# The code search reads x as loaded: the norm's scale goes into the codes of each sample, its shift into the row of code norms

## The chip, the cores and the metric

The kernel runs on one core of a Trainium2 chip. The metric is the device time of one execution in microseconds (us). An execution is timed as a whole; a profiled execution also shows every instruction of the five engines: TensorE (PE, with its weight loads shown apart as PEld), VectorE (DVE), ScalarE (ACT), GpSimd (POOL) and SyncE (SP), which here only issues DMAs.

## What is computed

The input x has 16 samples of 64 x 64 tokens with 256 channels, in f32. Four layers follow each other, each on the group norm of what the layer before left. The change touches the first one: each normed token is replaced by the nearest of 1024 code vectors, and that code is added to x.

```python
def _gn(v, G=32, eps=1e-5):
    g = v.reshape(B_, H_, W_, G, C_ // G)
    m = jnp.mean(g, axis=(1, 2, 4), keepdims=True)
    s = jnp.var(g, axis=(1, 2, 4), keepdims=True)
    return ((g - m) / jnp.sqrt(s + eps)).reshape(v.shape)
...
    dis = sum(xf * xf, axis=-1) + sum(embeddings * embeddings, axis=0) - 2.0 * matmul(xf, embeddings)
    indices = jnp.argmin(dis, axis=-1)
    quantized = jnp.take(embeddings.T, indices, axis=0)
...
    x = x + _L0_conv_ref(_gn(x), embeddings)
    x = x + _L1_conv_ref(_gn(x), ...)   # attention along rows, sigmoid
    x = x + _L2_conv_ref(_gn(x), ...)   # a gate by a softmax over 4096 x 4096 outer products
    x = x + _L3_conv_ref(_gn(x), ...)   # linear attention, then a layer norm
```

The norm is one scale s and one shift m for each sample and group of 8 channels, so a normed token is (x - m) s.

## The kernel before, in words

**Stages.** A sample passes through generators: `stats0` (loads the sample's x, channels on partitions, in 8 chunks of 512 tokens, and takes the norm's mean and variance), `stage1` (the search), `layer1`, `rows2`, `stage2` and `gate2` (the third layer), `stage3` (the fourth). A planner at the end of the file gives every generator a start time and a length in units of one sample and resumes, step by step, whichever is due first. In the middle of the run the search of one sample so lies beside the attention of the sample before, the exponentials of an earlier one, and so on. What the planner decides is the order in which the program names its instructions, which is their priority. A scheduler then gives each engine one fixed list; an engine takes its list strictly in order and waits where an operand is not there yet. Lines marked `tc.high_priority` are pulled ahead.

**The norm.** `gn_finish` ends every norm with a small chain: a weight on PE for the group means, the variance into `scale` on ACT (L276), minus the mean into `nmean` on ACT (L278), then on POOL the power -1/2 (L279) that makes `scale` the norm's s, and `nbias` = `nmean` x `scale` (L281). All three have one number for each channel.

**Constants.** The codes are loaded once into `e_raw` (256 x 1024 as two halves of 128 channels, 1 MB). ACT makes `e2`, twice the codes, which stays in SBUF for the whole run (L176); DVE and PE make `ne2`, minus the squared length of each code, repeated on all partitions.

**The search.** `stage1` goes through the 8 chunks. For a chunk, `load` fetches x (tile `xt`, three buffers); `norm` makes on ACT, for each half of the channels, the normed tile `xn` (L331) and its square `sq` (L334), then PE sums the squares of each token (L340), and after a copy on ACT (L345), a transpose (L347) and a copy on DVE (L352) minus the squared length of each token lies in `nx2`. For each of the 4 blocks of 128 tokens ACT writes `nn` = `ne2` + `nx2` (L381, 128 x 1024), PE multiplies `xn` with `e2` into the two-bank tile `pd` (L386, two halves of the codes times two halves of the channels), DVE adds the two and takes the maximum (L392), finds its place (L397), and POOL gathers that code from DRAM and adds it to the tokens (L398). `back` transposes the sum on PE (L361), ACT copies it over `xt` (L364), DVE takes the next norm's statistics, and the chunk is stored (L367). `norm` of a chunk is named after the third block of the chunk before, and `load` after its fourth block, two chunks ahead.

**Queues.** SP issues most loads and stores in one list, those of the search among them (L321, L325), and the loads of `stats0` (L302). Stores of `stage1` are issued by ACT.

Of the kernel before, what the change touches and what calls it, by code (L numbers as in the profile page):

```python
# [9 lines left out]
F32 = mybir.dt.float32  # L10
BF16 = mybir.dt.bfloat16
U32 = mybir.dt.uint32
AF = mybir.ActivationFunctionType
ALU = mybir.AluOpType
AX = mybir.AxisListType

P = 128
C = 256
NK = C // P
# [4 lines left out]
CW = CH * P  # L24
# [3 lines left out]
CODES = 1024  # L28
# [13 lines left out]
def kernel(  # L42
# [7 lines left out]
    nc = tc.nc  # L50
# [3 lines left out]
    const = ctx.enter_context(tc.tile_pool(name="const", bufs=1))  # L54
# [4 lines left out]
    s1p = ctx.enter_context(tc.tile_pool(name="s1p", bufs=2))  # L59
# [4 lines left out]
    dram = ctx.enter_context(tc.tile_pool(name="dram", bufs=2, space=bass.MemoryType.DRAM))  # L64
# [3 lines left out]
    def bank(name):  # L68
        return ps_m.tile([P, 512], F32, tag="pm", name=name)

    def wide(name):
        return ps_w.tile([P, 1024], F32, tag="pw", name=name)
# [99 lines left out]

    e_raw = s2p.tile([P, NK, CODES], F32, tag="x0b", name="e_raw", bufs=2)
    nc.sync.dma_start(out=e_raw, in_=emb.rearrange("(k p) n -> p k n", p=P))
    e2 = const.tile([P, NK, CODES], F32, name="e2")
    nc.scalar.mul(e2, e_raw, 2.0)  # L176
    e_sq = s2p.tile([P, NK, CODES], F32, tag="x2b", name="e_sq", bufs=2)
    nc.vector.tensor_tensor(e_sq, e_raw, e_raw, ALU.mult)
    ne2 = const.tile([P, CODES], F32, name="ne2")
    for hf in range(2):  # L180
        pe = bank(f"pe_{hf}")
        for k in range(NK):
            nc.tensor.matmul(
                pe, lhsT=neg_mat, rhs=e_sq[:, k, hf * 512 : (hf + 1) * 512],
                start=(k == 0), stop=(k == NK - 1),
            )
        nc.scalar.copy(ne2[:, hf * 512 : (hf + 1) * 512], pe)

    def load_wfg(t):
        nc.sync.dma_start(out=t[:, :, 0:CK], in_=wf.rearrange("(k p) n -> p k n", p=P))  # L190
        nc.sync.dma_start(out=t[:, :, CK : 2 * CK], in_=wg.rearrange("(k p) n -> p k n", p=P))
# [48 lines left out]
    for n in range(2):  # L240
        t = const.tile([P, CH, 2, ROW], F32, name=f"blk_{n}")
# [4 lines left out]
    for n in range(4):  # L246
        t = const.tile([P, 8], F32, name=f"m8_{n}")
# [4 lines left out]
    def stats_tile(kind, name):  # L252
        return small.tile([P, NK, NCHUNK, 6], F32, tag=f"gn_st{kind}", name=name, bufs=1)

    def chunk_stats(st, xt, ch):
        for k in range(NK):
            nc.vector.bn_stats(st[:, k, ch, :], xt[:, k, :])  # L257
# [33 lines left out]
                engine.tensor_scalar(v, v, scale[:, k : k + 1], None, ALU.mult)  # L291


    norm0 = {}

    def stats0(b):
        tag = f"s0_{b}"
        st = stats_tile(0, f"st_{tag}")
        src = xT[b].rearrange("(k p) n -> p k n", p=P)
        for ch in range(NCHUNK):  # L300
            xt = xb.tile([P, NK, CW], F32, tag="xb", name=f"xs_{tag}_{ch}")
            nc.sync.dma_start(out=xt, in_=src[:, :, ch * CW : (ch + 1) * CW])  # L302
            chunk_stats(st, xt, ch)
            yield 1.5
        with tc.high_priority(offset=URGENT):
            norm0[b] = gn_finish(st, "n0", b)
        yield 2


    x1_d, norm1 = {}, {}  # L310

    def stage1(b):
        tag = f"s1_{b}"
        scale, _, nbias = norm0.pop(b)
        src = xT[b].rearrange("(k p) n -> p k n", p=P)
        tok = x[b].rearrange("(t p) c -> p t c", p=P)
        xt, xc, xn, nx2, pxt = {}, {}, {}, {}, {}

        def load(ch):
            xt[ch] = xa.tile([P, NK, CW], F32, tag="xa", name=f"xt_{tag}_{ch}")  # L320
            nc.sync.dma_start(out=xt[ch], in_=src[:, :, ch * CW : (ch + 1) * CW])  # L321

        def tokens(ch):
            xc[ch] = s1p.tile([P, CH, C], F32, tag="xc", name=f"xc_{tag}_{ch}")
            nc.sync.dma_start(out=xc[ch], in_=tok[:, ch * CH : (ch + 1) * CH, :])  # L325

        def norm(ch):
            xn[ch] = s1p.tile([P, NK, CW], F32, tag="xn", name=f"xn_{tag}_{ch}")
            sq = s1p.tile([P, NK, CW], F32, tag="t4", name=f"sq_{tag}_{ch}", bufs=3)
            for k in range(NK):  # L330
                nc.scalar.activation(  # L331
                    xn[ch][:, k, :], xt[ch][:, k, :], AF.Identity, bias=nbias[:, k : k + 1], scale=scale[:, k : k + 1]
                )
                nc.scalar.activation(  # L334
                    sq[:, k, :], xt[ch][:, k, :], AF.Square, bias=nbias[:, k : k + 1], scale=scale[:, k : k + 1]
                )
            px = bank(f"px_{tag}_{ch}")
            for t in range(CH):
                for k in range(NK):
                    nc.tensor.matmul(  # L340
                        px[32 * t : 32 * t + 32, :P], lhsT=neg32, rhs=sq[:, k, t * P : (t + 1) * P],
                        start=(k == 0), stop=(k == NK - 1),
                    )
            xrow = small.tile([P, P], F32, tag="xrow", name=f"xrow_{tag}_{ch}", bufs=1)
            nc.scalar.copy(xrow, px[:, :P])  # L345
            pxt[ch] = bank(f"pxt_{tag}_{ch}")
            nc.tensor.transpose(pxt[ch][:, :P], xrow, ident)  # L347

        def norm_rows(ch):
            px = pxt.pop(ch)  # L350
            nx2[ch] = small.tile([P, CH], F32, tag="x2", name=f"nx2_{tag}_{ch}")
            nc.vector.tensor_copy(nx2[ch], px[:, :P].rearrange("p (t n) -> p t n", n=32)[:, :, 0])  # L352

        st1 = stats_tile(1, f"st1_{tag}")
        x1_d[b] = []

        def back(ch):
            for k in range(NK):
                pt = bank(f"pt_{tag}_{ch}_{k}")
                for t in range(CH):  # L360
                    nc.tensor.transpose(  # L361
                        pt[:, t * P : (t + 1) * P], xc[ch][:, t, k * P : (k + 1) * P], ident
                    )
                nc.scalar.copy(xt[ch][:, k, :], pt)  # L364
            chunk_stats(st1, xt[ch], ch)
            d = dram.tile([P, NK, CW], F32, tag=f"x1_{ch}", name=f"x1_{tag}_{ch}")
            nc.scalar.dma_start(out=d, in_=xt.pop(ch))  # L367
            x1_d[b].append(d)

        load(0)  # L370
        load(1)
        norm(0)
        norm_rows(0)
        tokens(0)
        yield 4
        for ch in range(NCHUNK):
            for t in range(CH):
                T = ch * CH + t

                nn = s1p.tile([P, CODES], F32, tag="t4", name=f"nn_{tag}_{T}", bufs=3)  # L380
                nc.scalar.activation(nn, ne2, AF.Identity, bias=nx2[ch][:, t : t + 1])  # L381
                pd = wide(f"pd_{tag}_{T}")
                for hf in range(2):
                    cols = slice(hf * 512, (hf + 1) * 512)
                    for k in range(NK):
                        nc.tensor.matmul(  # L386
                            pd[:, cols], lhsT=xn[ch][:, k, t * P : (t + 1) * P], rhs=e2[:, k, cols],
                            start=(k == 0), stop=(k == NK - 1),
                        )

                m8 = m8s[T % 4]
                nc.vector.tensor_tensor_reduce(  # L392
                    out=nn, in0=pd, in1=nn, scale=1.0, scalar=-3.0e38, op0=ALU.add, op1=ALU.max,
                    accum_out=m8[:, 0:1],
                )
                i8 = small.tile([P, 8], U32, tag="i8", name=f"i8_{tag}_{T}", bufs=4)
                nc.vector.max_index(i8, m8, nn)  # L397
                nc.gpsimd.indirect_dma_start(  # L398
                    out=xc[ch][:, t, :], out_offset=None,
                    in_=emb_rows, in_offset=bass.IndirectOffsetOnAxis(ap=i8[:, 0:1], axis=0),  # L400
                    compute_op=ALU.add,
                )
                yield 4
                if t == 1 and ch > 0:
                    back(ch - 1)
                    yield 2
                if t == 2 and ch + 1 < NCHUNK:
                    norm(ch + 1)
                    yield 2
                if t == 3:  # L410
                    if ch + 1 < NCHUNK:
                        norm_rows(ch + 1)
                        tokens(ch + 1)
                    if ch + 2 < NCHUNK:
                        load(ch + 2)
        back(NCHUNK - 1)
        with tc.high_priority(offset=URGENT):
            norm1[b] = gn_finish(st1, "n1", b)
        yield 3
# [492 lines left out]
    for _ in stats0(0):  # L912
        pass
    queue = [(start, n) for n, (start, _, _, _) in enumerate(tasks)]
    heapq.heapify(queue)
    while queue:
        now, n = heapq.heappop(queue)
        _, length, gen, total = tasks[n]
# [40 lines left out]
```

## Time and profile before

| | before |
|---|---|
| median of 3 executions | 5701.88 us (5696.69 to 5706.75) |
| the profiled execution | 5709.26 us |
| its span, first to last instruction | 5707.6 us |
| mean TensorE clock granted | 0.941 of full speed |
| moved by DMA | 991.87 MB, 174 GB/s on the mean |

How to read it: busy time is what the engine spent in instructions, without waiting; the mean of a group is the duration of one instruction, and since an instruction starts while the one ahead is still draining, the busy time of a group can be less than count times mean. "Idle before" is what the engine waited just ahead of a group, and behind the arrow stands who ended the wait. The chain of waits is followed back from the last instruction; in this profile its pieces reach back to about 1229 us from the start.

An f32 matmul of the source stands in the profile as two instructions: L386 is called 16 x 32 x 4 = 2048 times and has 4096 rows.

### The profile page before, as it was taken

What the parts mean: (1) busy time and instruction counts of PE and PEld (TensorE: products, weight loads), DVE (VectorE), ACT (ScalarE), POOL (GpSimd) and SP (SyncE); (2) the same over time, 40 slices, a digit from 0 to 9 for tenths busy, and PEclk for the clock granted to TensorE, in tenths of its full rate; (3) what the DMA queues carried; (4) which work ended last, traced back from release to release, by engine and by line L of the source; (5) the groups of instructions that cost most, each with busy time, mean ns of one, the idle gap of its engine ahead of it and who ended that gap; (6) DMA issues with size and microseconds to landing.
All of it is one profiled execution on the core that took longest, in us unless ns stands there. A gap on an engine that the chain in (4) does not pass through costs nothing.

```text
span 5707.6 us, 71918 instructions
## 1 busy us (share of the span) xinstructions
PE 5070.7 (89%) x24911; PEld 2999.1 (53%) x24911; DVE 5046.3 (88%) x7186; ACT 4578.7 (80%) x6578; POOL 1929.1 (34%) x1203
## 2 busy tenths in 40 slices
PE   8978899889999999999989999899999999997777
PEld 3534455445555565554645555564555545564444
DVE  6489798999999999998999999999898998988982
ACT  4478587978889798887978888798887878888873
POOL 3123233323333334334333333333333333321332
PEclk9988999989999999999999999999999999997888
DMA  6453835655666757566575756757475674745544
GB/s 187 141 158 93 265 112 188 176 161 177 191 188 176 212 160 198 175 190 186 170 205 163 187 188 177 203 161 218 143 193 172 184 207 142 203 153 160 158 137 92
DMA packets 453763, 991.87 MB, mean 174 GB/s; under 512 B 50456, under 2 KB 198808, under 8 KB 445208
## 3 DMA queue, kind: packets, MB, share of 16 engines
q1 hardware_dynamic: 320272, 750.88, 39.7%
q0 software_dynamic: 92160, 134.26, 15.5%
q10 hardware_dynamic: 40968, 102.13, 4.6%
q8 instruction: 198, 3.24, 0.2%
q14 instruction: 165, 1.35, 0.1%
HBM read 684.07 MB, written 303.04 MB: 173 GB/s over the span
## 4 chain that ended last, share of the span: by engine, by line
PE 34%; DVE 19%; ACT 13%; issue 6%; POOL 3%; DMA 3%; ACTq 0%; SPq 0%; POOLq 0%; DVEq 0%
PE pd_s L386 11%; DVE ex_s L631 7%; ACT ex_s L628 6%; PE ph_l L476 3%; DVE i_s L397 3%; PE pqv_s L762 2%; PE pxo_s L874 2%; PE pk_s L745 2%; ACT nn_s L381 2%; DVE nn_s L392 2%; POOL qv_s L780 1%; PE po_l L516 1%; PE pz_s L835 1%; DVE st_s L257 1%; DVE xg_g L686 1%
## 5 line engine op out<-in xcount | busy, mean ns | idle before, releaser
L631 DVE CUSTOM_DVE_ANT_0 ex_s<-ex_s,x2b 128x2048 f32<-128x2048 f32 x1024 | 2364.2, 2315 | 77.0 <-ACT ex_s L628 75.1
L628 ACT ACTIVATE ex_s<-x0b,nmax_s,x_r 128x2048 f32<-128x2048 f32 x1024 | 2137.9, 2088 | 80.8 <-DVE num_s L631 77.8
L386 PE MATMUL pd_s<-e,xn_s 128*128 128x512 f32 x4096 | 2008.5, 625 | 71.6 <-DVE m L392 61.5
L398 POOL DMA_INDIRECT xc_s<-in_emb_rows,i_s x512 | 1160.6, 2267 | 1794.2 <-DVE i_s L397 1255.3
L386 PEld LDWEIGHTS pd_s<-e,xn_s 128*128 128x128 f32 x4096 | 763.4, 198 | 855.4 <-issue 705.3
L392 DVE CUSTOM_DVE_ANT_0 nn_s<-pd_s,nn_s 128x1024 f32<-128x1024 f32 x512 | 619.7, 1213 | 137.4 <-PE pd_s L386 100.5
L381 ACT ACTIVATE nn_s<-ne,nx_s 128x1024 f32<-128x1024 f32 x512 | 580.4, 1143 | 55.9 <-DVE nx_s L352 27.5
L397 DVE FIND_INDEX8 i_s<-m,nn_s 128x8 uint32<-128x1024 f32 x512 | 623.5, 1219 | 0.0
L476 PE MATMUL ph_l<-wh_l,xt_l 128*128 128x256 f32 x2048 | 536.1, 399 | 68.0 <-DVE xt_l L521 42.6
L762 PE MATMUL pqv_s<-wqv_s,xk_s 128*128 128x256 f32 x2048 | 488.7, 380 | 0.0
L476 PEld LDWEIGHTS ph_l<-wh_l,xt_l 128*128 128x128 f32 x2048 | 386.6, 196 | 193.1 <-issue 65.9
L762 PEld LDWEIGHTS pqv_s<-wqv_s,xk_s 128*128 128x128 f32 x2048 | 388.7, 191 | 120.2 <-issue 59.8
L780 POOL TENSOR_TENSOR qv_s<-qv_s,qm_s 128x512 f32<-128x512 f32 x128 | 216.1, 1688 | 640.0 <-DVE qm_s L779 329.3
L874 PE MATMUL pxo_s<-qo_s,wctx_s 128*128 128x512 f32 x512 | 279.5, 630 | 18.5 <-DVE qo_s L854 18.1
L736 POOL TENSOR_TENSOR qv_s<-qv_s,qd_s 128x512 f32<-128x512 f32 x128 | 186.1, 1454 | 324.7 <-DVE qd_s L735 189.8
L516 PE MATMUL po_l<-blk,h_l 128*128 128x128 f32 x2048 | 286.1, 291 | 3.6 <-DVE m L392 2.9
L516 PEld LDWEIGHTS po_l<-blk,h_l 128*128 128x128 f32 x2048 | 263.1, 202 | 42.2 <-issue 22.8
L884 POOL DMA_DIRECT2D out<-y_s x128 | 118.9, 929 | 479.3 <-ACT lrs_s L845 235.2
L745 PE MATMUL pk_s<-xk_s,wk_s 128*128 128x512 f32 x512 | 259.0, 626 | 0.0
L846 POOL TENSOR_TENSOR lrs_s<-lrs_s,mhalf 128x4 f32<-128x4 f32 x128 | 199.0, 1555 | 173.1 <-ACT lrs_s L845 164.2
L361 PE MATMUL pt_s<-ident,xc_s 128*128 128x128 f32 x1024 | 157.6, 289 | 103.6 <-DMA xc_s<-in_emb_rows,i_s 70.0
L875 ACT ACTIVATE y_s<-pxo_s,xm_g 128x512 f32<-128x512 f32 x256 | 174.6, 683 | 91.3 <-PE pxo_s L874 90.6
(191 smaller groups left out, 7012.6 us busy)
## 6 DMA issues: line engine op xcount, KB each, us to landing
xs_s<-in_xT SPq DMA_DIRECT2D x128, 512.0 KB
xt_s<-in_xT SPq DMA_DIRECT2D x128, 512.0 KB
xc_s<-in_x SPq DMA_DIRECT2D x128, 512.0 KB
x_s<-xt_s ACTq DMA_DIRECT2D x128, 512.0 KB
xt_l<-x_s SPq DMA_DIRECT2D x128, 512.0 KB
x_l<-xt_l SPq DMA_DIRECT2D x128, 512.0 KB
xr_r<-x_l SPq DMA_DIRECT2D x128, 512.0 KB
xg_g<-x_l SPq DMA_DIRECT2D x128, 512.0 KB
```

Source lines behind the costliest of these rows:

```text
L381: nc.scalar.activation(nn, ne2, AF.Identity, bias=nx2[ch][:, t : t + 1])
L386: nc.tensor.matmul(pd[:, cols], lhsT=xn[ch][:, k, t * P : (t + 1) * P], rhs=e2[:, k, cols], start=(k == 0), stop=(k == NK - 1),)
L392: nc.vector.tensor_tensor_reduce(out=nn, in0=pd, in1=nn, scale=1.0, scalar=-3.0e38, op0=ALU.add, op1=ALU.max, accum_out=m8[:, 0:1],)
L397: nc.vector.max_index(i8, m8, nn)
L398: nc.gpsimd.indirect_dma_start(out=xc[ch][:, t, :], out_offset=None, in_=emb_rows, in_offset=bass.IndirectOffsetOnAxis(ap=i8[:, 0:1], axis=0),
L476: nc.tensor.matmul(ph[:, t, :], lhsT=X[:, k, t * P : (t + 1) * P], rhs=wh_n[:, k, :], start=(t % 2 == 0 and k == 0), stop=False, skip_grou ...
L516: nc.tensor.matmul(po[:, m : m + P], lhsT=h[:, t, k * P : (k + 1) * P], rhs=at[:, t, :, :].rearrange("p r i -> p (r i)"), start=True, stop ...
L628: nc.scalar.activation(ex, x0b, AF.Exp, bias=nmax[:, T : T + 1], scale=x01[:, T, 1:2], accum_out=den[:, h, T : T + 1])
L631: nc.vector.tensor_tensor_reduce(out=ex, in0=ex, in1=x2b, scale=1.0, scalar=0.0, op0=ALU.mult, op1=ALU.add, accum_out=num[:, h, T : T + 1],)
L745: nc.tensor.matmul(pk, lhsT=wk_n[:, k, :], rhs=xt[:, k, :], start=(k == 0), stop=(k == NK - 1))
L762: nc.tensor.matmul(pqv[:, j, :], lhsT=xt[:, k, t * P : (t + 1) * P], rhs=wqv_n[:, k, :], start=(j == 0 and k == 0), stop=False, skip_group ...
L874: nc.tensor.matmul(px, lhsT=wctx[:, 1, pr * P : (pr + 1) * P], rhs=qT, start=True, stop=True)
```

## The change

The search takes `xt`, x as loaded, as its stationary operand. With `ec` = 2 s e for each sample, the product with the normed x is x `ec` + `nmean` `ec`; the second part is a number for each code and is added to `ne2`, which makes the row `cn`. The squared lengths of the tokens are made as before, from `sq`.

- `e2` leaves SBUF. `e_raw` is doubled in place and stored once to DRAM (`e2_d`, issued by ACT).
- `scale_codes`, called in the last steps of `stats0`, loads `e2_d` into `ec` (1 MB, issued by SP; two buffers) and scales both halves on ACT.
- `code_row`, at the head of `stage1`, multiplies `nmean`, broadcast to 128 columns, with `ec` on PE (4 matmuls of 128 x 512) into two PSUM banks of the shared pool, and DVE adds `ne2` into `cn` (one buffer).
- The ACT instructions of L331 and the tile `xn` (two buffers of 512 KB) are gone.

```diff
-    e2 = const.tile([P, NK, CODES], F32, name="e2")
-    nc.scalar.mul(e2, e_raw, 2.0)
...
+    nc.scalar.mul(e_raw, e_raw, 2.0)
+    e2_d = dram.tile([P, NK, CODES], F32, tag="e2", name="e2_d", bufs=1)
+    nc.scalar.dma_start(out=e2_d, in_=e_raw)
...
+    def scale_codes(b):
+        tag = f"ec_{b}"
+        scale, nmean, _ = norm0[b]
+        ec = s1p.tile([P, NK, CODES], F32, tag="ec", name=tag)
+        nc.sync.dma_start(out=ec, in_=e2_d)
+        for k in range(NK):
+            nc.scalar.activation(ec[:, k, :], ec[:, k, :], AF.Copy, scale=scale[:, k : k + 1])
+        codes[b] = ec
+
+    def code_row(b):
+        tag = f"cn_{b}"
+        nmean, ec = norm0[b][1], codes[b]
+        cn = s1p.tile([P, CODES], F32, tag="cn", name=tag, bufs=1)
+        for hf in range(2):
+            cols = slice(hf * 512, (hf + 1) * 512)
+            pc = bank(f"p{tag}_{hf}")
+            for k in range(NK):
+                nc.tensor.matmul(
+                    pc, lhsT=nmean[:, k : k + 1].to_broadcast([P, P]), rhs=ec[:, k, cols],
+                    start=(k == 0), stop=(k == NK - 1),
+                )
+            nc.vector.tensor_tensor(cn[:, cols], pc, ne2[:, cols], ALU.add)
+        return cn
...
             norm0[b] = gn_finish(st, "n0", b)
-        yield 2
+        yield 1
+        scale_codes(b)
+        yield 1
...
+        cn, ec = code_row(b), codes.pop(b)
...
             for k in range(NK):
-                nc.scalar.activation(
-                    xn[ch][:, k, :], xt[ch][:, k, :], AF.Identity, bias=nbias[:, k : k + 1], scale=scale[:, k : k + 1]
-                )
                 nc.scalar.activation(
                     sq[:, k, :], xt[ch][:, k, :], AF.Square, bias=nbias[:, k : k + 1], scale=scale[:, k : k + 1]
                 )
...
-                nc.scalar.activation(nn, ne2, AF.Identity, bias=nx2[ch][:, t : t + 1])
+                nc.scalar.activation(nn, cn, AF.Identity, bias=nx2[ch][:, t : t + 1])
...
-                            pd[:, cols], lhsT=xn[ch][:, k, t * P : (t + 1) * P], rhs=e2[:, k, cols],
+                            pd[:, cols], lhsT=xt[ch][:, k, t * P : (t + 1) * P], rhs=ec[:, k, cols],
```

More of the change, by code (lines that the diff above doesn't have):

```diff
@@ L291, in scaled @@
                 engine.tensor_scalar(v, v, scale[:, k : k + 1], None, ALU.mult)
-    norm0 = {}
+    norm0, codes = {}, {}
+    def scale_codes(b):
[20 more added lines that the diff above has]
+        return cn
     def stats0(b):
@@ L316, in stage1 @@
         tok = x[b].rearrange("(t p) c -> p t c", p=P)
-        xt, xc, xn, nx2, pxt = {}, {}, {}, {}, {}
+        xt, xc, nx2, pxt = {}, {}, {}, {}
         def load(ch):
@@ L327, in norm @@
         def norm(ch):
-            xn[ch] = s1p.tile([P, NK, CW], F32, tag="xn", name=f"xn_{tag}_{ch}")
             sq = s1p.tile([P, NK, CW], F32, tag="t4", name=f"sq_{tag}_{ch}", bufs=3)
             for k in range(NK):
-                nc.scalar.activation(
-                    xn[ch][:, k, :], xt[ch][:, k, :], AF.Identity, bias=nbias[:, k : k + 1], scale=scale[:, k : k + 1]
-                )
                 nc.scalar.activation(
```

## The prediction

> **What bounds the kernel now.** I read three things in order: the busy shares, one long stretch in the middle, and the chain of waits through that stretch. First the shares of the whole span:
>
> ```profile
> PE 5070.7 (89%) x24911; PEld 2999.1 (53%) x24911; DVE 5046.3 (88%) x7186; ACT 4578.7 (80%) x6578; POOL 1929.1 (34%) x1203
> ```
>
> Three engines are nearly full. Next the table of stretches, whose columns are the length, then the busy time of PE, PEld, DVE, ACT and POOL, the granted clock, and DMA:
>
> ```profile
> 1500.00:4880.00 3380.00, 3109.56 (x15606) 1857.03 (x15606) 3136.08 (x4456) 2858.71 (x4109) 1243.43 (x741) 0.96 0.64 183
> ```
>
> This is ten samples at 338 us each. PE is at 92%, DVE at 93%, ACT at 85%: DVE idles 24 us per sample, PE 27, ACT 52. No engine is so full that its work alone sets the time. So I go to the chain of waits and add up its pieces between 1500 and 4880: PE 1481 us, DVE 862, ACT 576, 269 without a releaser, the rest POOL and DMA. Divided by the busy times above, a microsecond of work lies on the chain with 0.48 on PE, 0.27 on DVE and 0.20 on ACT. These three weights price work spread over the stretch. Work removed cannot be worth more than its own pieces on the chain until the order of the lists changes; work added at one place may cost all or nothing. I keep both as bounds.
>
> **What goes.** The normed tile is 256 ACT instructions. The groups (shapes, count, busy us, mean ns, idle time before and who ended it):
>
> ```profile
> L331 ACT ACTIVATE xn_s<-xt_s,nb_n,s_n 128x512 f32<-128x512 f32 x256 | 201.5, 806 | 41.5 <-DMA xt_s<-in_xT 24.8 <-PE pd_s L386 14.1 <-POOL nb_n L281 1.1
> L340 PE MATMUL px_s<-sq_s,neg 128*32 128x128 f32 x2048 | 120.2, 292 | 46.8 <-ACT sq_s L334 46.8
> L386 PE MATMUL pd_s<-e,xn_s 128*128 128x512 f32 x4096 | 2008.5, 625 | 71.6 <-DVE m L392 61.5 <-ACT xn_s L331 6.1 <-ACT h_l L485 2.2
> ```
>
> ACT loses 201.5 us of work, 12.6 per sample. By ACT's weight that is worth 0.20 x 201.5 = 40 us. The pieces of L331 that stand on the chain add up to only 17.4 us: mostly something else was as late. One such place, from the chain (start, us, what):
>
> ```profile
> 2033.87 0.82 ACT xn_s L331
> 2034.73 1.13 PE pd_s L386 x2
> ```
>
> The 14.1 us in which ACT waited for PE before it overwrote `xn` go too, but an idle ACT costs little: by its weight 3. What is late next? The matmuls of the search waited for `xn` only 6.1 us; the DVE maximum that frees their PSUM tile ended ten times as much idle time (61.5) and stays. The squares start one or two instructions sooner, since L331 stood ahead of them, and the sums of squares (L340), behind which PE idled 46.8 us, can gain up to that; but the list of PE is made anew, and will again put them close behind the squares. Between 17 and 43 I take the middle, **-30**.
>
> **What comes on PE.** 16 x 4 matmuls of 128 x 512 in f32. The profile splits each in two (L386: 2048 calls, 4096 rows), so 128 instructions. Their price is that of the search's own, which the chain shows eight at a time without a gap:
>
> ```profile
> 1950.81 3.63 PE pd_s L386 x8
> 1954.88 3.43 PE pd_s L386 x8
> ```
>
> That is 0.43 us each; with the mean over the run, 2008.5 / 4096, it is 0.49. So 55 to 63 us, I take 59, or 3.7 per sample. The broadcast stationary operand is no extra: L853 loads one too, and takes 142 ns against 198 in L386, under cover of the matmul ahead. The matmuls stand at the head of a sample, ahead of its first sums of squares and search matmuls, which wait behind them; `ec` and `nmean` have been ready for long by then, except in the first sample. If the 27 us in which PE idles per sample hid them all, they would cost nothing; if PE is the bound, 59. By the weight, 0.48 x 59 = **+28**.
>
> **What comes on DVE.** 32 additions from PSUM, 128 x 512. Nearest row, the same shape with one operand in PSUM:
>
> ```profile
> L837 DVE TENSOR_TENSOR qz_s<-pz_s,qo_s 128x512 f32<-128x512 f32 x128 | 88.0, 688 | 70.9 <-PE pz_s L835 68.2 <-ACT y_s L875 2.7
> ```
>
> 32 x 0.69 = 22 us; by the weight 0.27, **+6**, bounds 0 and 22. `cn` has one buffer, so an addition also waits for the last `nn` of the sample before; that `nn` runs on ACT ahead of the last maximum on DVE, which stands in front of the addition in the same list, so this wait is covered.
>
> **What comes on ACT and on the queues.** 32 scalings of 128 x 1024, priced by the writing of `nn`, which has the same size and also one operand per partition:
>
> ```profile
> L381 ACT ACTIVATE nn_s<-ne,nx_s 128x1024 f32<-128x1024 f32 x512 | 580.4, 1143 | 55.9 <-DVE nx_s L352 27.5 <-DVE i_s L397 26.6
> L557 ACT ACTIVATE wrow_n<-wrow_raw,s_n 128x12 f32<-128x12 f32 x32 | 8.0, 296 | 11.6 <-POOL s_n L279 11.4
> ```
>
> 32 x 1.13 = 36 us, by 0.20 **+7**. They add a wait: the scheduler puts them right behind the ACT instruction that feeds POOL's power (L276), so ACT stands until POOL answers, with the exponentials (L628) queued behind, and DVE waits for those. L557 waits in the same way for another norm, 11.4 us in 16 samples. I take that, 11 us, and by a weight between ACT's and one **+5**; if ACT waited as long as the longest landing of a 1 MB load on the chain (9.3 us, `x0b`) in every sample, it would be 149, which I hold for excluded in the middle, since the 1 MB load of `ec` is issued most of a sample ahead. That load waits on SP for the last search matmul of the sample before, and the loads behind it in SP's list wait too; it stands behind a load that already waits for the store of chunk 6, which needs gathers, transposes, copies and a store after all but the last search matmuls, so I take 0. 17 MB more on 992 are 1.7%, with the DMA engines 64% busy: 0.
>
> **The start.** Here nothing covers. The table of instructions in order of time (start, us, what):
>
> ```profile
> 22.95 1.10 SPq L321 DMA_DIRECT2D xt_s<-in_xT  x2
> 29.84 0.81 ACT L331 ACTIVATE xn_s<-xt_s,nb_n,s_n 128x512 f32<-128x512 f32 x1 [1.12 <-POOL nb_n L281]
> 38.58 1.23 DVE L392 CUSTOM_DVE_ANT_0 nn_s<-pd_s,nn_s 128x1024 f32<-128x1024 f32 x1 [1.28 <-ACT nn_s L381]
> ```
>
> Now the codes go through DRAM first. ACT's store stands behind small loads that it issues until 16 us and behind the doubling (1.9 us), so about 20; then a store and a load of 1 MB, about 6.5 each beside the chunks of x (the `x0b` loads on the chain take 5.5 to 9.3): 33. Scaling 2.3, the code row on PE 3.4, then sums of squares, transpose, `nn` as before (about 5 us): the first maximum at 44 in place of 38.6. **+5**, bounds 0 and 15.
>
> **Sum.** -30 + 28 + 6 + 7 + 5 + 5 = +21 us on the profiled execution of 5709.26, so 5730. The median of the runs is 7 us lower, 5701.88; with the same +21 it becomes **5723**.
>
> **A rule that weighs otherwise.** The Trainium skill, "Perfetto Trace Analysis", "Identifying the Most-Contended Engine", says to work on the engine with the highest occupancy, and to judge TensorE by its weight loads, since matmul busy time misleads. By weight loads PE is at 53% here, DVE is the engine, the code row on PE is free and the sum is -7. But the search matmuls come 0.43 us apart without a gap, so PE is truly occupied in these pieces, and I keep its weight. By either reading the engine that is relieved, ACT, is only the third.
>
> **Rivals.** (a) *Faster: ACT's relief counts full.* ACT ends about half of PE's idle time. If the pieces behind L331 give back 43 us and half of the 46.8 behind the squares, and the code row hides in PE's idle 27 us per sample at half its weight, the sum is -43 - 23 + 14 + 6 + 7 + 5 + 5 = -29: 5673. For it speaks PE's wait for the squares; against it, that L331 has only 17.4 us on the chain. It decides once the wait behind the squares shrinks by more than half.
> (b) *Slower: PE pays in full.* The code row opens each sample in a lump that all of the search waits behind, so 59 and not 28, and the removed work returns its 17: -17 + 59 + 6 + 7 + 5 + 5 = +65: 5767. It decides if PE's idle time per sample stays at 27 us. For it speaks PE's chain weight, the largest; against it, that gaps of PE lie all through the sample.
> (c) *The lists change more than the work.* All engines get new orders, and gains or losses of some 20 us to either side are possible without any of these causes. It widens all cases.
>
> **Chances.** The forecast 0.46, faster (a) 0.26, PE in full (b) 0.22, something worse, such as ACT held by the load of `ec`, 0.06. The forecast itself reaches from 5700 to 5745. A measurement of this kernel can tell about 0.2% from no change, 11 us. Faster than that: 0.27 (a and a little of the forecast); within: 0.21; slower: 0.52. The range, 5670 to 5772, goes from just under (a) to just over (b).
>
> **What would show it.** The L331 group gone; a PE group of 128 rows at 0.43 to 0.49 busy, a DVE group of 32 at 0.69, an ACT group of 32 at 1.13; the idle time behind the squares (46.8) down but not gone; the first maximum near 44 us; the ten samples in the middle at 339 instead of 338 us. If the middle is shorter, ACT's weight was set too low; if PE's idle time shrinks by the 3.7 per sample, the code row was hidden and my PE term was wrong.

## The result and the profile after

| | before | after |
|---|---|---|
| median, measured together, 13 executions each | 5703.58 us (5689.07 to 5719.81) | 5723.11 us (5713.4 to 5739.51) |
| ratio | | 1.0035, 95% interval 1.0023 to 1.0046 |
| the profiled execution, its span | 5709.26, 5707.6 | 5725.56, 5723.8 |
| TensorE clock | 0.941 | 0.951 |

The change costs 19.5 us. The forecast was 5723.0, +21 on the median. The number was met, by luck: the sections below show that the working under it mostly wasn't.

The busy shares of the changed kernel:

```profile
PE 5071.2 (89%) x25039; PEld 2983.9 (52%) x25039; DVE 5095.0 (89%) x7218; ACT 4438.8 (78%) x6354; POOL 1935.4 (34%) x1203
```

ACT lost 140 us of work. DVE gained 48.7, though its new additions take only 21. PE has 128 more instructions and the same busy time, to 0.5 us.

The stretch from 1500 to 4880, in the columns of before:

```profile
1500.00:4880.00 3380.00, 3101.73 (x15635) 1834.03 (x15634) 3157.59 (x4464) 2761.13 (x3958) 1262.62 (x740) 0.97 0.64 185
```

ACT idles 62 us a sample in place of 52, PE 28 as before (27), DVE 22 in place of 24.

The exponentials before, then the groups after that answer to those of before, and the new ones (operation, shapes, count, busy us, mean ns, idle time before and who ended it):

```profile
L628 ACT ACTIVATE ex_s<-x0b,nmax_s,x_r 128x2048 f32<-128x2048 f32 x1024 | 2137.9, 2088 | 80.8 <-DVE num_s L631 77.8
```

```profile
L652 ACT ACTIVATE ex_s<-x0b,nmax_s,x_r 128x2048 f32<-128x2048 f32 x1024 | 2137.6, 2088 | 121.3 <-DVE num_s L655 118.4 <-DVE nmax_s L639 0.5 <-issue 0.2
L410 PE MATMUL pd_s<-ec,xt_s 128*128 128x512 f32 x4096 | 1986.5, 621 | 79.9 <-DVE m L416 67.5 <-issue 11.3 <-ACT h_l L509 0.8
L405 ACT ACTIVATE nn_s<-cn,nx_s 128x1024 f32<-128x1024 f32 x512 | 581.1, 1144 | 103.0 <-DVE i_s L421 51.8 <-DVE nx_s L376 49.4
L364 PE MATMUL px_s<-sq_s,neg 128*32 128x128 f32 x2048 | 111.0, 285 | 47.4 <-ACT sq_s L358 47.0
L314 PE MATMUL pcn<-ec,nm_n 128*128 128x512 f32 x128 | 66.4, 663 | 4.0 <-ACT ec L303 4.0
L303 ACT ACTIVATE ec<-ec,s_n 128x1024 f32<-128x1024 f32 x32 | 35.2, 1140 | 19.4 <-POOL s_n L280 19.4
L318 DVE TENSOR_TENSOR cn<-pcn,ne 128x512 f32<-128x512 f32 x32 | 21.3, 676 | 14.6 <-PE pcn L314 14.6
```

The normed tile is gone. What ACT was spared became waiting: `nn` (L381 before, L405 now) waits 103.0 us in place of 55.9, the exponentials (L628 before, L652 now) 121.3 in place of 80.8, and both for DVE. PE's wait for the squares, which the prediction hoped to shorten, was 46.8 and is 47.4.

**Where the 20 us arise.** A mark that is easy to find in both traces is the first reduction over partitions on POOL (L612 before, L636 after), made once a sample. The first of them falls at 299.48 us before and 298.90 after. At the fourth mark, 1301 us before, the changed kernel is 3 us late, at the eighth (2636) 44, at the last (5276) 20. So it loses 41 us in four samples and wins 24 back in the rest. Here are two samples of each kernel (from and to, length, then the busy time of PE, PEld, DVE, ACT and POOL, clock, DMA share, GB/s). Before:

```profile
1633.88:1966.78 332.90, 310.97 (x1560) 185.34 (x1560) 315.27 (x447) 286.22 (x414) 124.72 (x75) 0.97 0.64 186
3985.62:4323.76 338.14, 308.67 (x1559) 184.67 (x1558) 312.76 (x448) 285.10 (x411) 120.98 (x74) 0.96 0.64 183
```

And after:

```profile
1648.16:1989.14 340.98, 310.91 (x1566) 183.57 (x1565) 320.11 (x448) 276.81 (x396) 128.08 (x75) 0.97 0.63 185
3690.67:4022.62 331.95, 305.93 (x1566) 181.09 (x1565) 314.20 (x447) 275.94 (x397) 128.26 (x74) 0.98 0.66 190
```

In the early sample the changed kernel is 8 us longer than the kernel before, and its DVE is busy 320 us with 448 instructions, where 447 take it 314 us in the late one.

The lists differ between the two halves. With the sample numbers taken out, the engine lists of samples 5 to 7 are alike, and so are those of 9 to 14, but the two patterns differ; they change over at sample 8, before the change and after. I call them order A and order B. The planner's due times are sums of many small floats; steps that should be due at the same moment are told apart by rounding, and that is what changes on the way.

**Two theories.** *Weights*, that of the prediction: work added or removed counts with its engine's share of the chain. *Lists*, the prediction's third rival made sharper: the change is worth little by itself, and the time follows the order in which it happens to leave the lists, which decides who meets whom.

### The profile page after: what moved, and what is told of

It is laid out like the page before. It is cut to its first block, busy times and chain, and to the rows that moved or that the text cites. A ratio compares the mean times of both kernels' runs of the same rounds, so it can differ in the third digit from the quotient of the medians.

```text
span 5723.8 us, 72183 instructions
## 1 busy us (share of the span) xinstructions
PE 5071.2 (89%) x25039; PEld 2983.9 (52%) x25039; DVE 5095.0 (89%) x7218; ACT 4438.8 (78%) x6354; POOL 1935.4 (34%) x1203
## 4 chain that ended last, share of the span: by engine, by line
PE 28%; DVE 22%; ACT 11%; issue 8%; DMA 5%; POOL 4%; ACTq 0%; SPq 0%; DVEq 0%; POOLq 0%
PE pd_s L410 10%; DVE ex_s L655 8%; ACT ex_s L652 4%; DVE i_s L421 3%; PE ph_l L500 3%; PE pxo_s L898 2%; DVE nn_s L416 2%; DMA xc_s<-in_emb_rows,i_s 2%; POOL qv_s L804 2%; PE pk_s L769 1%; DVE st_s L258 1%; PE pz_s L859 1%; DVE xg_g L710 1%; ACT nn_s L405 1%; DMA qo_s<-qd_s 1%
## 5 line engine op out<-in xcount | busy, mean ns | idle before, releaser
L655 DVE CUSTOM_DVE_ANT_0 ex_s<-ex_s,x2b 128x2048 f32<-128x2048 f32 x1024 | 2370.4, 2322 | 59.0 <-ACT ex_s L652 58.6
L652 ACT ACTIVATE ex_s<-x0b,nmax_s,x_r 128x2048 f32<-128x2048 f32 x1024 | 2137.6, 2088 | 121.3 <-DVE num_s L655 118.4
L410 PE MATMUL pd_s<-ec,xt_s 128*128 128x512 f32 x4096 | 1986.5, 621 | 79.9 <-DVE m L416 67.5
L422 POOL DMA_INDIRECT xc_s<-in_emb_rows,i_s x512 | 1135.5, 2218 | 1838.9 <-DVE i_s L421 1129.8
L410 PEld LDWEIGHTS pd_s<-ec,xt_s 128*128 128x128 f32 x4096 | 758.2, 198 | 856.6 <-issue 731.5
L416 DVE CUSTOM_DVE_ANT_0 nn_s<-pd_s,nn_s 128x1024 f32<-128x1024 f32 x512 | 618.7, 1213 | 131.8 <-PE pd_s L410 91.0
L405 ACT ACTIVATE nn_s<-cn,nx_s 128x1024 f32<-128x1024 f32 x512 | 581.1, 1144 | 103.0 <-DVE i_s L421 51.8
L804 POOL TENSOR_TENSOR qv_s<-qv_s,qm_s 128x512 f32<-128x512 f32 x128 | 215.2, 1682 | 666.4 <-DVE qm_s L803 393.6
L760 POOL TENSOR_TENSOR qv_s<-qv_s,qd_s 128x512 f32<-128x512 f32 x128 | 210.3, 1643 | 221.3 <-DVE qd_s L759 105.6
```

What stands on the lines that cost most here:

```text
L405: nc.scalar.activation(nn, cn, AF.Identity, bias=nx2[ch][:, t : t + 1])
L410: nc.tensor.matmul(pd[:, cols], lhsT=xt[ch][:, k, t * P : (t + 1) * P], rhs=ec[:, k, cols], start=(k == 0), stop=(k == NK - 1),)
L416: nc.vector.tensor_tensor_reduce(out=nn, in0=pd, in1=nn, scale=1.0, scalar=-3.0e38, op0=ALU.add, op1=ALU.max, accum_out=m8[:, 0:1],)
L422: nc.gpsimd.indirect_dma_start(out=xc[ch][:, t, :], out_offset=None, in_=emb_rows, in_offset=bass.IndirectOffsetOnAxis(ap=i8[:, 0:1], axis=0),
L652: nc.scalar.activation(ex, x0b, AF.Exp, bias=nmax[:, T : T + 1], scale=x01[:, T, 1:2], accum_out=den[:, h, T : T + 1])
L655: nc.vector.tensor_tensor_reduce(out=ex, in0=ex, in1=x2b, scale=1.0, scalar=0.0, op0=ALU.mult, op1=ALU.add, accum_out=num[:, h, T : T + 1],)
```

## The experiments

Each kernel was run beside the kernel before on the same chip; ratios are against it. In the three sets of runs the kernel before took 5710.51, 5713.55 and 5712.14 us.

**One part of the change at a time.** `t1_no_norm` is the kernel before without L331:

```diff
-                nc.scalar.activation(
-                    xn[ch][:, k, :], xt[ch][:, k, :], AF.Identity, bias=nbias[:, k : k + 1], scale=scale[:, k : k + 1]
-                )
...
-                            pd[:, cols], lhsT=xn[ch][:, k, t * P : (t + 1) * P], rhs=e2[:, k, cols],
+                            pd[:, cols], lhsT=xt[ch][:, k, t * P : (t + 1) * P], rhs=e2[:, k, cols],
```

> The kernel before without the normed tile: the search matmuls take x as loaded against the unscaled codes, so the norm is left out of the products (the squares keep it). Nothing is added. Theory of the weights (the prediction's terms, work priced by its share of the chain of waits): -30 us, between -17 and -43, against the kernel before, the gain spread evenly over the samples. Theory of the lists (the scheduler's new order of the lists outweighs the work): anything from -25 to +25, and unlike in the two stretches of the middle, 1300 to 2680 us and 3000 to 4700 us, where the planner's due times give two different repeating orders.

Measured 5689.30, ratio 0.9956 (0.994 to 0.9972), so -21 us by the medians and -25 by the ratio. The size fits the weights' term; the even spread does not. The mean sample is 0.5 us shorter than before between the fourth mark and the eighth and 1.4 between the ninth and the thirteenth, where 30 us on 16 samples ask for 1.9. The lists allow -25 as well, so this run does not decide between the two.

`t2_row_only` is the kernel before with the code row alone, made from `e2`:

```diff
...
+        cn = code_row(b)
...
-                nc.scalar.activation(nn, ne2, AF.Identity, bias=nx2[ch][:, t : t + 1])
+                nc.scalar.activation(nn, cn, AF.Identity, bias=nx2[ch][:, t : t + 1])
```

> The kernel before with the code row alone: 4 matmuls on PE and two additions on DVE per sample, made from the unscaled codes and added to the row of code norms, so the shift is put in twice. The normed tile stays. Theory of the weights: +34 us (28 for PE, 6 for DVE); PE in full +65 or more; hidden in PE's idle time 0 to +6. Theory of the lists: anything from -25 to +60, unlike in the two stretches.

Measured 5688.32, ratio 0.9955 (0.9938 to 0.9971): 22 us faster, with 64 us of matmuls more on PE and 21 us of additions on DVE. Over the whole run the weights' term fails, sign and all. The row is not free everywhere: in the four samples after the fourth mark it costs 3.3 us each, and DVE is 5 us busier in each (table below). The profiled execution wins 12 us before the fourth mark and 14 between the thirteenth and the last.

`t3_no_row` is the changed kernel without the row:

```diff
...
-        cn, ec = code_row(b), codes.pop(b)
+        ec = codes.pop(b)
...
-                nc.scalar.activation(nn, cn, AF.Identity, bias=nx2[ch][:, t : t + 1])
+                nc.scalar.activation(nn, ne2, AF.Identity, bias=nx2[ch][:, t : t + 1])
```

> The changed kernel without the code row: the shift is left out of the row of code norms. Theory of the weights: 34 us faster than the changed kernel, that is 14 us faster than the kernel before; and 16 us slower than the kernel that only drops the normed tile (scaling 7, wait for POOL 5, start 5). Theory of the lists: no such sum; the stretch from 1300 to 2680 us, where the changed kernel lost some 10 us per sample, moves by itself.

Measured 5706.93, ratio 0.9994 (0.9985 to 1.0004). Taken alone, this one agrees with the weights: the row seems to cost the changed kernel about 23 us. But the cost is not spread as work would be: without the row a sample takes 333.9 us in place of 344.0 in the stretch where the changed kernel lost its time, and 336.3 in place of 336.4 in the later one. That is what the lists let expect.

`t4_row_twice` is the changed kernel with every matmul of the row made twice:

```diff
-            for k in range(NK):
+            for k in (0, 1, 0, 1):
```

> The changed kernel with the matmuls of the code row done twice (the second pass starts the sum afresh, so the result is the same): 59 us more of PE work at the same place. Theory of the weights: +28 us against the changed kernel, +48 against the kernel before; PE in full +59 and +79; hidden: 0 and +20. Theory of the lists: no such order, from 0 to +60 against the changed kernel.

Measured 5710.47, ratio 0.9997 (0.9986 to 1.0007): faster than the changed kernel (1.0035) by some 20 us, with twice its row. More of the row's work on PE made nothing slower, so what the row costs is not priced by that work. The weights fall for PE. The lists had 0 to +60 against the changed kernel, so this result lies outside their range too.

**The same work in another order.** The next seven kernels differ from the two in the planner's arithmetic alone; no instruction is added or taken away. First the due times as exact fractions, and then all of them 16 higher, where floats are coarser; each gives one order from sample 5 to 14, neither A nor B:

```diff
...
-            heapq.heappush(queue, (now + length * step / total, n))
+            heapq.heappush(queue, (now + length * exact(step) / total, n))
```

```diff
-    queue = [(start, n) for n, (start, _, _, _) in enumerate(tasks)]
+    queue = [(start + 16, n) for n, (start, _, _, _) in enumerate(tasks)]
```

> The kernel before, its planner's due times kept as exact fractions of 1/10000 in place of floats. No instruction is added or removed; ties among due times are broken the same way in every sample, so that samples 5 to 14 all get one relative order of the engine lists, where the kernel before has one order for samples 5 to 7 and another for 9 to 14. Theory of the weights (work added or removed, priced by its engine's share of the chain): no work has changed, so 0, within 5 us of the kernel before. Theory of the lists (the order in which the instructions meet, DVE's and POOL's stretched operations above all, is worth as much as the change itself): another time, anywhere within 30 us to either side, one steady period from sample 5 to 14, and DVE's busy time per sample moving with that period at an unchanged number of instructions.

> The changed kernel with the same exact fractions in the planner; no instruction is added or removed. Theory of the weights: 0 against the changed kernel, so 15 to 25 us over the kernel before, and as much over the kernel before with exact fractions. Theory of the lists: the changed kernel lost 10 us a sample in samples 5 to 8 only, in which its DVE was busy 320 us a sample in place of 314; with another order of the lists the loss should go away or spread over all samples, so a difference to the kernel before with exact fractions that is off 20 us by 15 us or more.

> The kernel before, every due time of the planner 16 higher, so that its floats round as in later samples and all samples get a third order of the lists. No instruction is added or removed. Theory of the weights: 0, within 5 us of the kernel before. Theory of the lists: another time, within 30 us to either side.

> The changed kernel, every due time of the planner 16 higher; no instruction is added or removed. Theory of the weights: 0 against the changed kernel, and 15 to 25 us over the kernel before with the same shift. Theory of the lists: a difference to the kernel before with the same shift that is off 20 us by 15 us or more, and may have the other sign.

Then both kernels held in order A, by rounding all times to one grid (start at 4, steps of 2^-50), and the changed one in order B (start at 8, steps of 2^-49):

```diff
-    queue = [(start, n) for n, (start, _, _, _) in enumerate(tasks)]
+    def grid(v):
+        return Fr(round(Fr(v) * 2 ** 50), 2 ** 50)
+
+    queue = [(grid(start + 4), n) for n, (start, _, _, _) in enumerate(tasks)]
...
-            heapq.heappush(queue, (now + length * step / total, n))
+            heapq.heappush(queue, (grid(now + Fr(length * step / total)), n))
```

> The kernel before, no instruction added or removed. The planner's due times start at 4 and are rounded to one grid, so that the order in which the kernel before runs samples 5 to 7 (order A: 332 to 337 us a sample there) is kept from sample 5 to 14, where the kernel before goes over to another (order B: 334 to 346 us a sample). Theory of the lists: 332 to 337 us a sample throughout, so some 20 to 35 us faster than the kernel before. Theory of the weights: no work changed, within 5 us of it.

> The changed kernel in order A from sample 5 to 14, no instruction added or removed. Theory of the lists: the 341 to 346 us a sample that it took in samples 5 to 8 now last to the end, 45 to 60 us over the changed kernel, and 75 to 110 us over the kernel before in order A. Theory of the weights: as the changed kernel, 15 to 25 us over the kernel before in order A.

> The changed kernel in order B from sample 5 to 14, no instruction added or removed. Theory of the lists: the 332 to 342 us a sample that it took from sample 9 on now hold from sample 5, so 25 to 40 us under the changed kernel and 5 to 25 us under the kernel before: the same change, faster. Theory of the weights: as the changed kernel, 15 to 25 us over the kernel before.

| order of the lists | kernel before, us | changed kernel, us | the change |
|---|---|---|---|
| as the planner leaves it | 5703.58 | 5723.11 | +19.5 |
| exact fractions | 5738.44, ratio 1.0048 (1.003 to 1.0065) | 5782.48, ratio 1.0124 (1.0103 to 1.0146) | +44 |
| 16 higher | 5763.62, ratio 1.0097 (1.0078 to 1.0117) | 5740.08, ratio 1.0054 (1.0033 to 1.0076) | -24 |
| A throughout | 5680.26, ratio 0.9949 (0.993 to 0.9968) | 5778.85, ratio 1.0122 (1.0099 to 1.0146) | +99 |
| B throughout | not run | 5703.09, ratio 0.9982 (0.9963 to 1.0001) | |

Each row compares kernels measured together. With no work changed, the kernel before moves over 83 us and the changed one over 79, four times the effect of the change, whose sign goes with the order. The list theory's numbers were met for A: the kernel before 32 us faster (20 to 35 expected), the changed one 67 slower than the kernel before and 99 slower than it in order A (75 to 110). For B it is 20 us under the changed kernel by the medians and 30 by the ratios, where 25 to 40 were expected, and 9 under the kernel before, which its interval just fails to tell from none. The kernel before in order A beats both kernels. Two of the list theory's expectations were missed: with times 16 higher the kernel before lost 50 us, where at most 30 were expected, and with exact fractions its sample grew to 339.5 us while DVE's busy time, which was to move with it, stayed at 313.3.

The mean length of a sample from those marks, and DVE's mean busy time in it, in two stretches of four samples each:

| kernel | mark 4 to 8 | DVE | mark 9 to 13 | DVE |
|---|---|---|---|---|
| before (A, then B) | 333.7 | 313.2 | 336.8 | 312.4 |
| after (A, then B) | 344.0 | 320.4 | 336.4 | 315.0 |
| before, A throughout | 333.8 | 313.7 | 335.5 | 313.9 |
| after, A throughout | 344.3 | 319.9 | 342.4 | 320.7 |
| after, B throughout | 335.7 | 314.4 | 335.9 | 314.2 |
| before, exact fractions | 339.5 | 313.3 | 337.2 | 313.2 |
| after, exact fractions | 342.8 | 317.2 | 343.4 | 317.9 |
| before, 16 higher | 338.5 | 313.0 | 340.4 | 313.5 |
| after, 16 higher | 339.2 | 315.9 | 337.9 | 316.0 |
| before, no normed tile | 333.2 | 313.3 | 335.4 | 313.5 |
| before, row alone | 337.0 | 318.3 | 336.4 | 313.4 |
| after, no row | 333.9 | 312.6 | 336.3 | 313.4 |
| after, row twice | 340.6 | 313.7 | 336.1 | 315.7 |

Each line is one profiled execution. The fastest and the slowest of the 13 executions before lie 31 us apart, 2 us a sample, so a single difference of that size says little.

In order B no cost of the change is seen. In order A it costs 10 us a sample, and 7 of them are DVE's: 1.3 are the row's own additions, 3.6 the gate multiply and 2.1 the product of the exponentials. The kernels with one part of the change show where it comes from: the row alone brings a part of it, the changed kernel without the row none. In the later stretch the row's matmuls cost nothing that can be seen, whether added to the kernel before (336.8 to 336.4), taken from the changed one (336.4 to 336.3) or doubled (336.1), where the weight asked for 1.8 us a sample each time. One of these differences alone would say little; the three agree.

**What meets in order A.** The groups of DVE that differ, in one sample of the kernel before:

```profile
L631 DVE CUSTOM_DVE_ANT_0 ex_s<-ex_s,x2b 128x2048 f32<-128x2048 f32 x64 | 148.4, 2322 | 3.7 <-ACT ex_s L628 3.7
L686 DVE SCALAR_TENSOR_TENSOR xg_g<-xg_g,nm_n,u_g 128x512 f32<-128x512 f32 x16 | 12.7, 816 | 0.0
```

and after, in order A:

```profile
L655 DVE CUSTOM_DVE_ANT_0 ex_s<-ex_s,x2b 128x2048 f32<-128x2048 f32 x64 | 149.3, 2338 | 1.6 <-ACT ex_s L652 1.6
L710 DVE SCALAR_TENSOR_TENSOR xg_g<-xg_g,nm_n,u_g 128x512 f32<-128x512 f32 x16 | 16.7, 1062 | 0.0
```

The gate multiply (L710) took 4 us more. Its instructions one by one show why. In the whole changed kernel 206 of the 256 run without a POOL operation on `qv` beside them and take 0.68 to 0.75 us; the other 50 take 1.52 on the mean and up to 2.85. The product of the exponentials (L655) takes 2.22 to 2.31 us in 876 cases without such an operation, and 2.58 on the mean and up to 4.45 in the 148 beside one. Some instructions of DVE and POOL in the same 27 us of the changed kernel (start, us, what):

```profile
1711.79 2.35 DVE L710 SCALAR_TENSOR_TENSOR xg_g<-xg_g,nm_n,u_g 128x512 f32<-128x512 f32 x1
1715.20 0.74 DVE L710 SCALAR_TENSOR_TENSOR xg_g<-xg_g,nm_n,u_g 128x512 f32<-128x512 f32 x1
1721.86 2.90 DVE L655 CUSTOM_DVE_ANT_0 ex_s<-ex_s,x2b 128x2048 f32<-128x2048 f32 x1 [0.44 <-ACT ex_s L652]
1732.84 2.27 DVE L655 CUSTOM_DVE_ANT_0 ex_s<-ex_s,x2b 128x2048 f32<-128x2048 f32 x1
1735.30 2.86 DVE L655 CUSTOM_DVE_ANT_0 ex_s<-ex_s,x2b 128x2048 f32<-128x2048 f32 x1
```

```profile
1711.91 1.67 POOL L804 TENSOR_TENSOR qv_s<-qv_s,qm_s 128x512 f32<-128x512 f32 x1
1721.56 1.05 POOL L760 TENSOR_TENSOR qv_s<-qv_s,qd_s 128x512 f32<-128x512 f32 x1 [2.58 <-DVE qd_s L759]
1732.93 3.10 POOL L804 TENSOR_TENSOR qv_s<-qv_s,qm_s 128x512 f32<-128x512 f32 x1 [1.45 <-DVE nx_s L376]
```

The gate multiply that starts at 1711.79 has 1.67 of its 2.35 us beside POOL's subtraction (until 1713.58); the 0.68 us outside it are close to the 0.74 of the next one, with POOL silent. It goes the other way too. POOL's subtraction (L804) takes 1.04 to 1.05 us in the 57 cases with neither of the two DVE instructions beside it. The one at 1732.93 starts just behind a product and takes 3.10: that product keeps its 2.27, and the next takes 2.86. POOL's multiplication at 1721.56 (L760) starts ahead of a product: it takes 1.05, and the product 2.90. The profile counts the stretch as busy time, so no table of waits shows it.

`f4_after_pool_small` cuts the work of these two POOL operations to a sixteenth:

```diff
-            nc.gpsimd.tensor_tensor(q4, q4, qd.unsqueeze(3).to_broadcast([P, CH, HEADS, DH]), ALU.mult)
+            q1 = q4[:, 0, 0, :]
+            nc.gpsimd.tensor_tensor(q1, q1, qd[:, 0, 0:1].to_broadcast([P, DH]), ALU.mult)
...
-            nc.gpsimd.tensor_tensor(q4, q4, qm.unsqueeze(3).to_broadcast([P, CH, HEADS, DH]), ALU.subtract)
+            q1 = q4[:, 0, 0, :]
+            nc.gpsimd.tensor_tensor(q1, q1, qm[:, 0, 0:1].to_broadcast([P, DH]), ALU.subtract)
```

> The changed kernel, with the two operations of POOL on qv (a subtraction and a multiplication on 128 x 512) cut to 128 x 32, which leaves out 15 of 16 parts of the softmax over q; their waits stay. The lists of samples 5 to 7 are the same but for some ten instructions; after sample 8 they are others, so only samples 5 to 8 are compared. If DVE lost its 7 us a sample there (320 busy in place of 313) because its two-input operations met POOL's on qv: the gate multiply falls from 1060 ns to some 720, the product of the exponentials from 2340 to 2280 ns or less, DVE's busy time to 311 to 314, and the period from 344 us to 335 to 338. If DVE's stretched operations have another cause: no change there. If they do, but don't set the time: DVE's busy time falls and the period stays at 341 or more.

Measured 5658.19, ratio 0.9906 (0.9882 to 0.993). The sample of order A and the two groups in it:

```profile
1636.41:1970.90 334.49, 308.91 (x1569) 183.03 (x1568) 311.71 (x448) 276.44 (x396) 119.10 (x75) 0.98 0.64 189
```

```profile
L655 DVE CUSTOM_DVE_ANT_0 ex_s<-ex_s,x2b 128x2048 f32<-128x2048 f32 x65 | 147.7, 2277 | 1.4 <-ACT ex_s L652 1.4
L710 DVE SCALAR_TENSOR_TENSOR xg_g<-xg_g,nm_n,u_g 128x512 f32<-128x512 f32 x16 | 11.6, 748 | 0.1
```

DVE's two groups are no longer stretched. POOL's small operations still are: 0.24 us as a rule without one of the two DVE instructions beside them, up to 2.92 with one, and POOL's busy time on `qv` falls only from 30.3 to 21.3 us a sample.

Over the four samples DVE's busy time falls from 320.4 to 311.1 and the period from 344.0 to 335.1, and DVE's idle time stays at 24 us. So the stretch of DVE comes from these POOL operations, and with it goes what order A had cost the changed kernel. The run does not separate all of it: it takes 9.3 us from DVE, more than the 7 that the change had added there, and it shortens POOL's work too. Nor does the period follow DVE in every order: with the row twice DVE is back at 313.7 us, and a sample still takes 340.6. How much the kernel before would gain by the same cut was not tried.

They are not all that an order does. In the kernel before with times 16 higher, DVE is busy 313 us and the gate multiply takes its usual 12.7 us, yet a sample takes 338 to 340. There it is waiting. The group of DVE that scales a weight by the norm, in the kernel before and then in that one:

```profile
L291 DVE TENSOR_SCALAR wh_l<-wh_l,s_n 128x256 f32<-128x256 f32 x32 | 10.3, 360 | 20.6 <-POOL s_n L279 20.6
```

```profile
L291 DVE TENSOR_SCALAR wh_l<-wh_l,s_n 128x256 f32<-128x256 f32 x32 | 10.3, 363 | 50.8 <-POOL s_n L279 50.8
```

DVE waits 30 us more for POOL's power, and the profiled span is 31 longer (5739.0 against 5707.6). I read the one as the cause of the other, without a run that takes this wait away; it is not shown. Other waits of DVE moved nearly as much (its maximum's for the search matmuls fell from 100.5 to 74.4 us, its statistics' for the copy over `xt` rose from 20.9 to 44.1), and the medians lie 50 us apart, not 31. Why the changed kernel with the row twice needs 340.6 us in its early samples, at 313.7 us of DVE, stays open.

## Why the prediction was right in its number, and where its working failed

- **The normed tile, -30.** Near in size: -21 to -25 in `t1_no_norm`. That the size comes from ACT's relief is not shown: the gain is not spread over the samples, and an order alone moves the kernel before by more. The squares' wait (46.8) did not shrink: 50.3 in `t1_no_norm`, 47.4 in the changed kernel. By its own condition rival (a) is out.
- **The code row on PE, +28.** This is the step that failed: "By the weight, 0.48 x 59 = +28". The duration was a little short: 66.4 us for 128, where 55 to 63 were forecast, 0.52 us each, and the weight load of the broadcast operand took 213 ns, not 142. The price was wrong. Adding the row alone gave -22, doubling it -13 (by the medians) to -22 (by the ratios) against the changed kernel. The run without the row is the one in which the row looks dear (+23), and there the cost lies in the samples of order A, where DVE met POOL. The chain passed through PE for 1481 of 3380 us, but the row's work on PE lengthened no sample of the later stretch, so here a share of the chain was no price for new work on that engine. Rival (b), with the full 59, falls with it, although its own sign, PE's idle time staying at 27 us a sample, came. The sign that the prediction named for this error, PE's idle time going down by 3.7 us a sample, did not appear (27.0 us before, 27.8 after, over 1500 to 4880), and yet the term was wrong. Neither sign could tell: PE's busy time is not a sum of fixed durations (last section).
- **DVE's additions, +6.** 21.3 us of work as forecast (22), 676 ns each for 688. What was missed is that DVE's other operations would grow: by 27 us over the run, 5.7 us a sample in order A.
- **ACT's scaling, +7, and its wait, +5.** 35.2 us for 36; the wait is 19.4 us for 11. No run priced them alone. `t3_no_row` minus `t1_no_norm` (17.6 us) holds them, the start and the order together.
- **The start, +5.** The first maximum was to come at 44 us and did:

```profile
43.87 1.22 DVE L416 CUSTOM_DVE_ANT_0 nn_s<-pd_s,nn_s 128x1024 f32<-128x1024 f32 x1 [0.64 <-PE pd_s L410]
```

  But at the first mark both kernels are level (299.48 and 298.90): 300 us later the delay is not seen. The first mark moves between 294 and 308 us among the kernels of this document, so a start of 5 us is lost in that.
- **SP and DMA, 0.** No sign against it.
- **The middle.** From the fourth mark to the thirteenth the sample grew from 335.9 to 339.6 us, by 3.7 where 1 was forecast. And it is no steady 3.7: +10 in the four samples of order A, and -0.4 in four of order B.
- **Rival (c), the lists change more than the work.** This was the true mechanism. The prediction priced it at 20 us to either side and used it only to widen the cases. It measured 80 us for either kernel. That the sum of the terms came to +21 and the planner's own order to +19.5 is luck, an agreement of two numbers that have little to do with each other; in the other orders the same terms would have missed by 23, 45 and 78 us.
- **The rule of the Trainium skill** ("Perfetto Trace Analysis", "Identifying the Most-Contended Engine") pointed at DVE, with the row on PE free. (Beside the weight loads the page names the matmuls' share of the peak rate, which the prediction did not work out.) On the row it was nearer than the weights. Its sum of -7 missed too, since DVE's loss came by meetings with POOL that no share of busy time shows.

## What to carry to other kernels

Where an order made by a planner fills three engines to nine tenths, first run the unchanged kernel in two or three equivalent orders: that spread (80 us here) is the error of a prediction that leaves the order out, and choosing the best order was worth more (32 us) than this change. Compare the busy time of groups that the change did not touch: when it grows at the same count, look for another engine's instruction beside the long ones. A share of the chain tells where time was spent, not what more work there will cost.

## What the hardware showed

- **DVE and POOL stretch each other.** In the changed kernel, the gate multiply: 0.68 to 0.75 us, up to 2.85 beside an operation of POOL on `qv`; the product of the exponentials: 2.22 to 2.31, up to 4.45; POOL's subtraction on `qv`: 1.04 to 1.05, up to 3.22. All three read two operands in SBUF. The maximum (L416), one operand in PSUM and one in SBUF, took 1.17 to 1.23 us in the 54 cases beside such an operation, as it does without. The Trainium skill, "GPSIMD Engine Reference", section "Key points", says that GpSimd shares its SBUF interfaces with VectorE and that they contend when a VectorE instruction has two SBUF inputs. The trace agrees.
- **PE's busy time is not additive.** 128 matmuls of 66 us left it at 5071 us, while the granted clock went from 0.941 to 0.951 and the search's own matmuls from 2008.5 to 1986.5 us. With the row twice, another 128, it is 5115.8 at 0.951:

```profile
PE 5115.8 (89%) x25167; PEld 3005.4 (53%) x25167; DVE 5074.8 (89%) x7218; ACT 4439.4 (78%) x6354; POOL 1928.6 (34%) x1203
```

  Busy time times clock goes 4772, 4823, 4865: it rises by 51 and 42 with each 128. The order moves this product as well: it is 4763 to 4801 in the six kernels without the row, 4809 to 4856 in the seven that make it once. So the first step is clear of the order, the second hardly. What sets the granted clock was not tried.
